# A two-layer graph attention kernel on one core: edge rows moved behind one-hots and merge on VectorE, and layer 1's gathered rows scaled chunk by chunk on ScalarE

## The chip, the core and the metric

One core of a Trainium2 chip. The metric is device time in microseconds of one execution; lower is better. The runs shown are whole executions, and the profile is one further execution of the same program.

## The reference

6250 nodes with 256 features, 200000 edges sorted by destination, 32 features an edge. A layer norm with relu, then two graph attention layers (4 heads of 64, then 1 head of 256) with self loops, and residual additions:

```python
def _gat(x, src, dst, ea, Wg, a_s, a_d, Wge, a_e, b, n, h, f):
    hx = (x @ Wg).reshape(n, h, f)
    he = (ea @ Wge).reshape(-1, h, f)
    al = leaky_relu(einsum('nhf,hf->nh', hx, a_s)[src] + einsum('nhf,hf->nh', hx, a_d)[dst]
                    + einsum('ehf,hf->eh', he, a_e), 0.2)
    m = segment_max(al, dst, num_segments=n)
    al = exp(al - m[dst])
    al = al / segment_sum(al, dst, num_segments=n)[dst]
    out = segment_sum(hx[src] * al[:, :, None], dst, num_segments=n)
    return out.reshape(n, h * f) + b

h = maximum(_layernorm(x), 0)
te = relu(edge_attr @ We0 + be0) * exp(h @ Wo0 + bo0)[src][:, None]
y = relu(_gat(h, *with_self_loops(src, dst, te), layer 0 weights) + h)
te = relu(edge_attr @ We1 + be1) * exp(y @ Wo1 + bo1)[src][:, None]
z = _gat(y, *with_self_loops(src, dst, te), layer 1 weights) + y
return x + (z + h)
```

## The kernel before

A prologue computes, per node, a table row for layer 0: the 256 projected features, the attention terms and the edge gate. Then the edges run in steps of 24 chunks of 128 edges, 66 steps a layer (the last two are shorter), first all of layer 0, then all of layer 1. Layer 0's node work writes the table that layer 1 gathers from.

All engines run lists written out by hand: each engine executes in the order in which `edges` issues, and waits only for what the data need. One pass of the loop in `edges` (line 668) handles step `st` and prepares the next one, `nx`:

- `gather(nx)`, line 871: 24 indirect DMAs issued by POOL, one a chunk, each bringing 128 table rows into `G`, a buffer of [128, 24, 270]. There are three of them, used in turn.
- `logits(st)`, lines 1071 to 1088 on VectorE: the first line that reads the gathered rows; it adds the edge terms from `rt` and `ade`, takes the leaky relu, and scans for the maximum of each segment. `ends` and `links` (lines 1099 to 1116) carry the maxima across rows.
- `spread`, `parts`, `blocks`, `rphase1`, `rphase2`, `adst` of `nx`: the edge network on TensorE and ScalarE (lines 968, 969, 977), and the destination's term (1029, 1043); the result stands in the PSUM tile `zad`.
- `maxima(st)`, lines 1126 to 1149: the softmax weights. ScalarE's Exp (line 1145) writes them to `k_w`, a part of the PSUM tile `kps`; VectorE copies them into `G` (line 1149).
- `scale(st)`, line 1180: VectorE multiplies all 24 gathered rows of `G`, 6144 elements a partition, by the weights in `k_w` (the 128 partitions hold 128 edges of each chunk).
- `carried(st)`, lines 1162 to 1170: VectorE adds, in row 0 of chunk 0, what a destination has from the step before (its tile `U`).
- `sums(st)`, line 1192: TensorE adds up the scaled rows by destination with one-hot matrices `S`, one fp32 multiplication a chunk, into the PSUM tile `u`. `evict(st)` (line 1197) copies it to `U` on ScalarE.
- `edge_rows(nx)`, lines 1057 and 1060: VectorE turns `zad` into `rt` by a transpose and reduces `ade` from it; the next step's `logits` read both.
- `onehots(nx)`, lines 1005 and 1008: VectorE compares, 3072 elements a partition, for the next `S`.
- `finish(pv)`: the merge of the step before with the self loop and the node's own values, on VectorE with one or two short ScalarE instructions: `nodes1` in layer 1 (lines 1213 to 1228 with the Exp in line 1222, then 1305 and 1307), `nodes0` in layer 0 (lines 1208 to 1242, then 1265 to 1279).
- `index_on`: in some passes, indices for later steps on VectorE (lines 602 to 633).

The order on VectorE around the change, in one pass:

```python
            drain(self.scale(st))
            self.carried(st)
            self.sums(st)
            if late:
                self.rows3(late)
                late = None
            self.edge_rows(nx)
            self.onehots(nx)
            if pv:
                drain(self.finish(pv))
            self.evict(st)
```

The last three steps of a layer are issued by `ending`, an order of its own; the pass before it (the one with `st["s"] + 4 == self.NS`) also finishes its own step.

Of the kernel before, what the change touches and what calls it, by code (L numbers as in the profile page):

```python
# [22 lines left out]
F32 = mybir.dt.float32  # L23
BF = mybir.dt.bfloat16
I32 = mybir.dt.int32
AF = mybir.ActivationFunctionType
# [5 lines left out]
P = 128  # L32
C = 24
SE = P * C
NX = 24
D = 256
# [43 lines left out]
class Kernel:  # L80
# [556 lines left out]
    def edges(self, ctx):  # L637
        nc = self.nc
        self.gp += [self.pool(f"gath{i}", 1, ctx) for i in range(1, 3)]
        self.sp = self.pool("onehot", 2, ctx)  # L640
        self.wp = self.pool("work", 2, ctx)
        self.np_ = self.pool("nodes", 2, ctx)
        self.xp = self.pool("index", 1, ctx)
        self.ps_y = self.pool("ps_y", 1, ctx, space=PSUM)
        self.ps_1 = self.pool("ps_1", 1, ctx, space=PSUM)
        self.ps_f = self.pool("ps_f", 1, ctx, space=PSUM)
        self.lf = self.ps_1.tile([P, 512], F32, name="lf")
        nc.vector.memset(self.lf[0:4, 0:1], -BIG)
        steps = self.steps
        self.state = {0: None, 1: None}  # L650
        self.nodes(steps[0])
        self.gather(steps[0])
        if self.NS % 2:
            self.load_lb(1)
        self.spread(steps[0])
        self.parts(steps[0])
        self.blocks(steps[0])
        drain(self.rphase1(steps[0]))
        self.load_ea(1)
        self.rphase2(steps[0])  # L660
        self.adst(steps[0])
        self.onehots(steps[0])
        drain(self.soon)
        self.edge_rows(steps[0])

        pv = late = None
        self.ahead, self.rest = 1, None
        for k, st in enumerate(steps):
            nx = steps[k + 1] if k + 1 < len(steps) else None
            if st["s"] + 2 >= self.NS:  # L670
                continue
            for q in steps[k + 1:k + 3]:
                if q["L"] is st["L"] and "tw" not in q:
                    self.nodes(q)
            self.load_lb(k + 2)
            left = 99
            if self.ahead < len(self.groups):
                left = self.groups[self.ahead][0] - 2 - (self.ahead + 2 >= len(self.groups)) - k
            if self.rest is None and left <= 2:
                gi = self.index_load(self.ahead, self.xp)  # L680
                self.rest = self.index_group(self.ahead, self.xp, gi)
            if st["s"] + 3 == self.NS:
                self.ending(st, *steps[k + 1:k + 3], pv, late, steps[k + 3] if k + 3 < len(steps) else None)
                pv = late = None
                continue
            self.gather(nx)
            drain(self.logits(st))
            self.ends(st)
            self.spread(nx)
            self.parts(nx)  # L690
            y = self.rphase1(nx)
            next(y)
            self.links(st)
            if late:
                self.rows2(late)
            self.load_fl(k + 1)
            self.blocks(nx)
            drain(self.maxima(st))
            drain(y)
            self.load_ea(k + 2)  # L700
            self.rphase2(nx)
            self.adst(nx)
            if "S" not in st:
                self.onehots(st)
            drain(self.scale(st))
            self.carried(st)
            self.sums(st)
            if late:
                self.rows3(late)
                late = None  # L710
            self.edge_rows(nx)
            self.onehots(nx)
            if pv:
                drain(self.finish(pv))
            self.evict(st)
            if pv:
                self.rows1(pv)
                late = pv
            self.index_on(left)
            if st["s"] + 4 == self.NS:  # L720
                drain(self.finish(st))
            if k >= 6:
                next(self.late, None)
                next(self.late, None)
            pv = st
        self.flag()

# [390 lines left out]
    def maxima(self, st):  # L1118
        nc, L, c, o, pc = self.nc, st["L"], st["C"], st["o"], st["pc"]
        H, G = L.H, st["G"]  # L1120
        V = nc.vector
        m = self.wp.tile([P, 4 * C], F32, name="m")
        t = self.mt
        n = H * c
        mh = m[:, :n].rearrange("p (h c) -> p h c", c=c)
        V.tensor_tensor(st["four"][:, :, n:2 * n].rearrange("p i (h c) -> p i h c", c=c),  # L1126
                        self.flpen[:, :, o:o + c].unsqueeze(2).to_broadcast([P, 2, H, c]),
                        self.lf[:, 160:224].rearrange("p (i h) -> p i h", i=2)[:, :, :H].unsqueeze(3)
                        .to_broadcast([P, 2, H, c]), op=OP.add)
        yield  # L1130
        V.tensor_reduce(m[:, :n], st["four"][:, :, :2 * n].rearrange("p i (j n) -> p n i j", j=2),  # L1131
                        axis=AX.XY, op=OP.max)
        yield
        V.tensor_sub(t[:, :n], st["al"][:, :n], m[:, :n])
        yield
        if st["prev"] is not None:
            pr = t[0:1, n:n + H]
            if H == 1:
                V.tensor_scalar(pr, pc[0:1, 0:H], mh[0:1, :, 0], -1e4, op0=OP.subtract, op1=OP.max)
            else:  # L1140
                V.tensor_sub(pr, pc[0:1, 0:H], mh[0:1, :, 0])
                yield
                V.tensor_scalar(pr, pr, -1e4, None, op0=OP.max)
            yield
        nc.scalar.activation(self.k_w[:, :n + H], t[:, :n + H], AF.Exp)
        V.tensor_tensor(G[:, :c, L.m:L.m + H].rearrange("p c h -> p h c"), mh,
                        self.isl[:, o:o + c].unsqueeze(1).to_broadcast([P, H, c]), op=OP.mult)
        yield
        V.tensor_copy(G[:, :c, L.p:L.p + H].rearrange("p c h -> p h c"),
                      self.k_w[:, :n].rearrange("p (h c) -> p h c", c=c))  # L1150
        yield
        st["pr"] = self.k_w[0:1, n:n + H]

    def carried(self, st):

# [17 lines left out]
    def scale(self, st, cuts=(0, C)):  # L1173
        nc, L, c = self.nc, st["L"], st["C"]
        H, G = L.H, st["G"]
        pw = self.k_w[:, :H * c].rearrange("p (h c) -> p c h", c=c)
        for c0, c1 in zip(cuts, cuts[1:]):
            c1 = min(c, c1)
            v = G[:, c0:c1, 0:D].rearrange("p c (h f) -> p c h f", h=H)
            nc.vector.tensor_tensor(v, v, pw[:, c0:c1, :].unsqueeze(3)  # L1180
                                    .to_broadcast([P, c1 - c0, H, L.F]), op=OP.mult)
            yield

    def sums(self, st, *parts):
        nc, L, c = self.nc, st["L"], st["C"]
        G, S = st["G"], st["S"]
        for a, b in parts or ((0, c),):
            for i in range(a, b):
                j = st["n"] = st.get("n", -1) + 1
                if j == 0:  # L1190
                    st["u"] = self.ps_1.tile([P, 512], F32, name="u")
                nc.tensor.matmul(st["u"][:, :L.W], S[:, i, :], G[:, i, 0:L.W], start=(j == 0), stop=(j == c - 1))  # L1192
# [263 lines left out]
def drain(g):  # L1456
    for _ in g:
        pass
# [93 lines left out]
```

## Time and profile before

| | us |
|---|---|
| median of 3 runs | 4064.29 |
| lowest and highest | 4062.84, 4064.88 |
| the profiled execution, its own time | 4068.59 |
| its span, first to last instruction | 4066.2 |

How to read the lines: a group of instructions is given by line of the kernel, engine, operation and tiles (out<-in), shapes, count; then busy time in us and the mean of one in ns; then the engine's idle time just before these instructions and what ended it. A line of the timeline gives start, duration (us), then the same names, and in brackets the idle time before it with what released it. Two rows on one engine may overlap, since instructions are pipelined. A line of a query by source line gives the least, median and largest duration in ns. A line of the stages gives the stretch, its length, POOL's busy time and count, then the granted TensorE clock, the DMA share and GB/s. PE is TensorE, PEld its weight load, DVE VectorE, ACT ScalarE, POOL GpSimd, SP SyncE.

### The profile page before, as it was taken

To read this page: it belongs to the slowest core of one execution; us is meant where nothing else is said; L and a number is where in the kernel's file an instruction comes from. 1 tells how busy PE (TensorE), PEld (TensorE's weight loads), DVE (VectorE), ACT (ScalarE), POOL (GpSimd) and SP (SyncE) were. 2 spreads that over 40 slices of the span, in tenths; PEclk is the share of its full clock that TensorE was granted. 3 is DMA by queue.
4 is the path that set the end of the run, shared out by engine and by line. 5 is a ranking of instruction groups with operands and counts; after the bars stand their busy time and mean duration, and the time that the engine had idled before them with its cause. 6 is when DMAs were issued, how large, how long until landed. Compare 5 with 4: busy or idle time off the path is not lost.

```text
span 4066.2 us, 34155 instructions
## 1 busy us (share of the span) xinstructions
PE 2696.3 (66%) x9878; PEld 1737.4 (43%) x9878; DVE 2855.0 (70%) x6188; ACT 519.9 (13%) x1158; POOL 3012.7 (74%) x3255
## 2 busy tenths in 40 slices
PE   8776666666666766766646656666657666666665
PEld 6454444444444444444433433433434334334334
DVE  7887877877877877777856656656566566565666
ACT  5211111111111111111110000000000000000000
POOL 5777777777777777777747777777777777777775
PEclk9888888887887788888777787777777777777777
DMA  7455555555555555555434455455455445445443
GB/s 251 137 152 140 146 149 140 145 149 144 142 150 147 140 148 147 141 147 148 134 103 133 136 142 141 130 141 140 132 140 140 134 137 143 132 137 142 132 137 96
DMA packets 231085, 576.17 MB, mean 142 GB/s; under 512 B 63097, under 2 KB 87871, under 8 KB 230825
## 3 DMA queue, kind: packets, MB, share of 16 engines
q0 software_dynamic: 150144, 422.75, 39.6%
q1 hardware_dynamic: 80331, 150.52, 11.4%
q8 instruction: 79, 1.29, 0.1%
q14 instruction: 115, 0.94, 0.1%
q10 hardware_dynamic: 416, 0.67, 0.1%
HBM read 542.72 MB, written 31.09 MB: 141 GB/s over the span
## 4 chain that ended last, share of the span: by engine, by line
POOL 53%; issue 19%; DVE 19%; DMA 4%; PE 4%; ACT 1%; SPq 0%; DVEq 0%; ACTq 0%; POOLq 0%
POOL G L871 53%; DVE G L1180 6%; DMA G<-T,src 4%; DVE S L1008 3%; DVE lb L992 1%; PE ps L444 1%; PE y L968 1%; PE u L1192 1%; DVE rt L1057 1%; DVE m L1131 1%; DVE ade L1060 0%; DVE G L1169 0%; DVE fb L1126 0%; DVE al L1075 0%; DVE al L1073 0%
## 5 line engine op out<-in xcount | busy, mean ns | idle before, releaser
L871 POOL DMA_INDIRECT G<-T,src x3102 | 2959.9, 954 | 1001.1 <-issue 929.7
L1192 PE MATMUL u<-G,S 128*128 128x270 f32 (+1 forms) x6252 | 1617.9, 423 | 250.8 <-DVE G L1170 247.2
L1192 PEld LDWEIGHTS u<-G,S 128*128 128x128 f32 x6252 | 1295.4, 209 | 585.6 <-DVE G L1170 314.7
L1180 DVE TENSOR_TENSOR G<-G,kps 128x6144 f32<-128x6144 f32 (+2 forms) x140 | 853.3, 6099 | 0.0
L1071 DVE TENSOR_TENSOR G<-rt,G 128x96 f32<-128x96 f32 (+1 forms) x132 | 30.3, 229 | 910.3 <-DMA G<-T,src 910.0
L1099 PE MATMUL lf<-ident,fb 128*36 128x128 f32 (+1 forms) x132 | 49.5, 375 | 710.8 <-DVE fb L1088 684.3
L1008 DVE TENSOR_TENSOR S<-kps,loc 128x3072 f32<-128x3072 f32 x132 | 437.5, 3315 | 4.6
L968 PE MATMUL y<-ea,webd 64*128 64x256 f32 (+1 forms) x1056 | 396.7, 846 | 51.4 <-ACT R L969 51.4
L977 PE MATMUL zad<-R,wea 128*64 128x384 f32 (+1 forms) x1056 | 301.2, 711 | 158.4 <-ACT R L969 158.1
L969 ACT ACTIVATE R<-y,webd 128x1024 f32<-128x1024 f32 (+2 forms) x264 | 235.6, 892 | 1226.0 <-PE y L968 741.5
L1099 PEld LDWEIGHTS lf<-ident,fb 128*36 128x36 f32 (+1 forms) x132 | 15.6, 118 | 752.5 <-DVE fb L1088 725.2
L977 PEld LDWEIGHTS zad<-R,wea 128*64 128x64 f32 x1056 | 86.7, 185 | 426.0 <-ACT R L969 340.6
L968 PEld LDWEIGHTS y<-ea,webd 64*128 64x128 f32 x1056 | 125.6, 291 | 125.5 <-ACT R L969 70.4
L1197 ACT ACTIVATE U<-u 128x270 f32<-128x270 f32 (+1 forms) x132 | 51.9, 394 | 645.9 <-PE u L1192 645.9
L1029 PE MATMUL zad<-a,Q 128*128 128x12 bf16 (+1 forms) x132 | 26.1, 198 | 160.1 <-DVE a L1024 160.1
L444 PE MATMUL fin<-wg,h1T 128*128 128x260 f32 x264 | 128.7, 638 | 3.7 <-ACT h1T L1287 3.7
L1057 DVE STREAM_TRANSPOSE rt<-zad 128x768 f32<-128x768 f32 (+1 forms) x130 | 124.5, 957 | 5.1 <-PE zad L1043 5.1
L992 DVE TENSOR_TENSOR lb<-lb,kps 128x1536 bf16<-128x1536 bf16 (+1 forms) x68 | 113.5, 1670 | 0.0
L1222 ACT ACTIVATE mw<-mw,mg 128x2 f32<-128x2 f32 x66 | 19.7, 298 | 623.9 <-DVE mg L1221 623.9
L1029 PEld LDWEIGHTS <-Q 128*128 128x128 bf16 x132 | 16.0, 121 | 172.7 <-DVE a L1024 165.8
L1043 PE MATMUL zad<-lb,aq 128*128 128x384 bf16 (+1 forms) x264 | 86.5, 421 | 0.0
L444 PE MATMUL ps<-wg,hT 128*128 128x266 f32 x292 | 83.2, 410 | 1.7 <-ACT hT L326 1.6
(190 smaller groups left out, 2109.8 us busy)
## 6 DMA issues: line engine op xcount, KB each, us to landing
G<-T,src POOLq DMA_INDIRECT x3102, 2.8
ea<-in_ea_dram SPq DMA_DIRECT2D x64, 768.0 KB
lb<-locrow SPq DMA_DIRECT2D x64, 384.0 KB
T<-t1row SPq DMA_DIRECT2D x66, 227.5 KB
tw<-T SPq DMA_DIRECT2D x66, 225.8 KB
tw<-T SPq DMA_DIRECT2D x66, 117.2 KB
tw<-in_x_dram SPq DMA_DIRECT2D x66, 112.0 KB
out_dram<-fb SPq DMA_DIRECT2D x64, 112.0 KB
```

Source lines behind the costliest of these rows:

```text
L444: self.nc.tensor.matmul(ps[:, :L.MW], hT[:, k, :], self.wg[L.l][:, k, :], start=(k == 0), stop=(k == 1))
L871: nc.gpsimd.indirect_dma_start(out=G[:, c, 0:L.TW], out_offset=None, in_=self.rows[L.l][0:n * (1 + L.l), :], in_offset=bass.IndirectOffset ...
L968: nc.tensor.matmul(y[:, i, :n], self.webd[l][r, :], ea[r, w], start=True, stop=True)
L969: nc.scalar.activation(R[:, :, w], y[:, :, :n], AF.Relu, bias=self.be[l])
L977: nc.tensor.matmul(st["zad"][i * PH:(i + 1) * PH, o], self.wea[l][0], R[:, i, w], start=True, stop=False)
L992: V.tensor_tensor(lb[:, :, :n], lb[:, :, :n], self.k_part.unsqueeze(2).to_broadcast([P, i, n]), op=OP.is_equal)
L1008: nc.vector.tensor_tensor(st["S"][:, c0:c1, :], self.k_iota.unsqueeze(1).to_broadcast(w), self.loc[:, o + c0:o + c1].unsqueeze(2).to_broad ...
L1043: self.nc.tensor.matmul(st["zad"][:, o], st["aq"].rearrange("p k j -> p (k j)"), st["lb"][:, w], start=False, stop=True)
L1057: V.transpose(rv[:, :32 * c].rearrange("p (b n) -> p b n", b=2), z.rearrange("p (b n) -> p b n", b=2)[:, :, :16 * c])
L1099: self.nc.tensor.transpose(self.lf[0:e.shape[1], 1:P + 1], e, self.ident)
L1180: nc.vector.tensor_tensor(v, v, pw[:, c0:c1, :].unsqueeze(3) .to_broadcast([P, c1 - c0, H, L.F]), op=OP.mult)
L1192: nc.tensor.matmul(st["u"][:, :L.W], S[:, i, :], G[:, i, 0:L.W], start=(j == 0), stop=(j == c - 1))
```

## The change

Two things. In layer 1, in all steps but those of `ending`, the weights go to a tile `kw` in SBUF instead of `k_w` in PSUM, and ScalarE multiplies the gathered rows, one instruction of 128x256 a chunk with the chunk's column of `kw` as its scale, in place of VectorE's one instruction. And in both layers `edge_rows(nx)` is issued behind the one-hots, the merge of `pv`, the eviction and the index work; in the pass ahead of `ending` that step's own merge follows it.

```diff
             self.gather(nx)
+            st["rows"] = st["L"].l
             drain(self.logits(st))
...
-            drain(self.scale(st))
+            if st["rows"]:
+                self.scale_rows(st)
+            else:
+                drain(self.scale(st))
             self.carried(st)
             self.sums(st)
             if late:
                 self.rows3(late)
                 late = None
-            self.edge_rows(nx)
             self.onehots(nx)
             if pv:
                 drain(self.finish(pv))
...
             self.index_on(left)
-            if st["s"] + 4 == self.NS:
-                drain(self.finish(st))
             if k >= 6:
                 next(self.late, None)
                 next(self.late, None)
+            self.edge_rows(nx)
+            if st["s"] + 4 == self.NS:
+                drain(self.finish(st))
             pv = st
...
-        nc.scalar.activation(self.k_w[:, :n + H], t[:, :n + H], AF.Exp)
+        k_w = self.k_w
+        if st.get("rows"):
+            st["w"] = k_w = self.wp.tile([P, C + 1], F32, name="kw")
+        nc.scalar.activation(k_w[:, :n + H], t[:, :n + H], AF.Exp)
...
         V.tensor_copy(G[:, :c, L.p:L.p + H].rearrange("p c h -> p h c"),
-                      self.k_w[:, :n].rearrange("p (h c) -> p h c", c=c))
-        yield
-        st["pr"] = self.k_w[0:1, n:n + H]
+                      k_w[:, :n].rearrange("p (h c) -> p h c", c=c))
+        yield
+        st["pr"] = k_w[0:1, n:n + H]
...
+    def scale_rows(self, st):
+
+        G = st["G"]
+        for c in range(st["C"]):
+            v = G[:, c, 0:D]
+            self.nc.scalar.activation(v, v, AF.Copy, scale=st["w"][:, c:c + 1])
```

## The prediction

> **What bounds the kernel now.** I read the page's busy shares first, then the groups of instructions by line with what ended the idle time before them, then the stages, and then the timeline of one step of each layer.
>
> ```profile
> PE 2696.3 (66%) x9878; PEld 1737.4 (43%) x9878; DVE 2855.0 (70%) x6188; ACT 519.9 (13%) x1158; POOL 3012.7 (74%) x3255
> ```
> ```profile
> POOL G L871 53%; DVE G L1180 6%; DMA G<-T,src 4%; DVE S L1008 3%; DVE lb L992 1%; PE ps L444 1%; PE y L968 1%; PE u L1192 1%; DVE rt L1057 1%; DVE m L1131 1%; DVE ade L1060 0%; DVE G L1169 0%; DVE fb L1126 0%; DVE al L1075 0%; DVE al L1073 0%
> ```
> ```profile
> L871 POOL DMA_INDIRECT G<-T,src x3102 | 2959.9, 954 | 1001.1 <-issue 929.7 <-DMA T<-t1row 40.5 <-DMA T<-trow 12.5
> L1180 DVE TENSOR_TENSOR G<-G,kps 128x6144 f32<-128x6144 f32 (+2 forms) x140 | 853.3, 6099 | 0.0
> L1071 DVE TENSOR_TENSOR G<-rt,G 128x96 f32<-128x96 f32 (+1 forms) x132 | 30.3, 229 | 910.3 <-DMA G<-T,src 910.0
> ```
> ```profile
> L871 POOL DMA_INDIRECT G<-T,src x3102: 942/947/1197, 88.8 to 4036.3; - x194
> ```
>
> By busy share three engines look alike. The groups part them. Nearly all of POOL's idle time before a gather, 929.7 of 1001.1 us, is "issue": 0.30 us each, POOL's own way from one gather to the next. The rest is mainly the two waits for tables (40.5 between the layers, 12.5 at the start). VectorE on the other hand stands 910 us at L1071, the first line that reads gathered rows, until a gather lands. The account closes: 88.8 us before the first gather, 2959.9 + 1001.1 - 12.5 for the gathers (the 12.5 lies in the 88.8), 29 from the last one (4036.3) to 4066.2, together 4066. So the time is 3102 gathers at 954 + 300 ns, a head, a wait between the layers and a tail. DVE, ACT and PE decide only in the last three, or where they reach POOL.
>
> **The change, part by part.** Here is a step of layer 1.
>
> ```profile
> 3012.05 0.20 DVE L1071 TENSOR_TENSOR G<-rt,G 128x24 f32<-128x24 f32 x1 [10.01 <-DMA G<-T,src]
> ...
> 3016.05 0.20 ACT L1145 ACTIVATE kps<-mt 128x25 f32<-128x25 f32 x1 [0.30 <-DVE mt L1139]
> ...
> 3016.38 6.55 DVE L1180 TENSOR_TENSOR G<-G,kps 128x6144 f32<-128x6144 f32 x1
> ...
> 3017.93 1.11 ACT L969 ACTIVATE R<-y,webd 128x1024 f32<-128x1024 f32 x1 [1.68 <-PE y L968]
> ...
> 3021.85 0.82 PE L1043 MATMUL zad<-lb,aq 128*128 128x384 bf16 x2
> ...
> 3022.96 0.48 DVE L1162 SCALAR_TENSOR_TENSOR G<-U,kps,G 1x257 f32<-1x257 f32 x1
> ...
> 3023.49 0.96 DVE L1057 STREAM_TRANSPOSE rt<-zad 128x768 f32<-128x768 f32 x1
> ...
> 3023.62 12.58 PE L1192 MATMUL u<-G,S 128*128 128x261 f32 x48 [0.95 <-DVE G L1170]
> 3024.49 0.23 DVE L1060 TENSOR_REDUCE ade<-rt 128x24 f32<-128x72 f32 x1
> 3024.64 0.15 DVE L1005 COPY kps<-lastloc 128x1 f32<-128x1 f32 x1
> ...
> 3024.82 3.36 DVE L1008 TENSOR_TENSOR S<-kps,loc 128x3072 f32<-128x3072 f32 x1
> ...
> 3029.05 0.30 ACT L1222 ACTIVATE mw<-mw,mg 128x2 f32<-128x2 f32 x1 [10.01 <-DVE mg L1221]
> ...
> 3029.38 0.22 DVE L1224 SCALAR_TENSOR_TENSOR mg<-U,mw 128x1 f32<-128x1 f32 x1 [0.37 <-ACT mw L1222]
> ...
> 3030.61 0.48 DVE L1307 SCALAR_TENSOR_TENSOR fb<-tw,mw,fb 128x256 f32<-128x256 f32 x1
> ...
> 3036.24 0.39 ACT L1197 ACTIVATE U<-u 128x261 f32<-128x261 f32 x1 [6.90 <-PE u L1192]
> ...
> 3040.30 0.20 DVE L1071 TENSOR_TENSOR G<-rt,G 128x24 f32<-128x24 f32 x1 [9.20 <-DMA G<-T,src]
> ...
> 3048.56 1.11 ACT L969 ACTIVATE R<-y,webd 128x1024 f32<-128x1024 f32 x1 [1.77 <-PE y L968]
> ```
>
> *Removed:* one L1180 of 6.55 us in each of layer 1's 63 ordinary steps (66 less the three that the end handles by itself), 412 us of VectorE. None of it is worth anything directly: behind it VectorE waits for a gather all the same, 10.01 us in the row above, 9.20 in the next. That wait becomes longer.
>
> *Added:* 63 x 24 = 1512 scalings of 128x256 on ScalarE, which reads one per-row factor. The trace has no such instruction. Its neighbours, the first without and the second with two per-row operands:
>
> ```profile
> L1271 ACT ACTIVATE fb<-fb 128x256 f32<-128x256 f32 x66 | 27.5, 417 | 129.2 <-DVE fb L1269 129.2
> L1253 ACT ACTIVATE hw<-tw 128x256 f32<-128x256 f32 x66 | 38.6, 585 | 0.2 <-issue 0.2
> ```
> ```profile
> 1001.59 0.40 ACT L1197 ACTIVATE U<-u 128x270 f32<-128x270 f32 x1 [4.14 <-PE u L1192]
> 1001.88 0.38 ACT L1287 ACTIVATE h1T<-fin 128x256 f32<-128x256 f32 x1
> ```
>
> One operand stands half way, 0.50 us. Two that follow each other overlap by 0.11 us (1001.59 + 0.40 against 1001.88), so I take a row each 0.39 to 0.40 us and 0.585 as the upper bound: 9.6 us a step, at most 14.0. The Trainium skill (ScalarE: Activation LUTs, "What ACT_TABLE_LOAD costs") gives 186 ns plus 0.833 ns an element, 93 ns more for each pointer operand and 93 ns of overlap; as an estimate from that page a row would be 0.49 us and a step 9.6, which the trace's neighbours bear out.
>
> The rows queue behind ScalarE's L969, which ends at 3019.04, so they end at 3028.6 (bound: 3033.1). The first is done near 3019.5 and lets L1162 go 3.4 us earlier than now. PE gains less: its L1043 runs until 3022.67 in front of the sums, so they start 0.9 us earlier; PE needs 12.58 us for them, more than ScalarE needs for the rows, and ends about 3035.3 (by the bound no later than 3034 + the last chunk). U is then copied a little earlier than at 3036.24, and G comes free no later.
>
> *The new wait:* L1222 stands behind the 24 rows on ScalarE, and VectorE waits for it at L1224. Queued there are the rest of the merge and, now, the edge rows. The merge ends 1.7 us after L1224 starts (L1307 ends 3031.09) and the edge rows take 1.15 us (3023.49 to 3024.64). VectorE is then through at 3028.6 + 0.3 + 2.9, about 3032, at most 3036.4. The next gather lands for 3040.3: a margin of 8 us, at worst 4. It costs nothing.
>
> *Moved:* edge rows, in both layers. L1057 and L1060 issue no DMA and pass nothing on SP or POOL; they pass one-hots, merge and the index work on VectorE, and in the last ordinary step they go ahead of that step's own merge, which waits for U anyway. In layer 0 the same work is done later in the same step, in front of an idle stretch:
>
> ```profile
> 1018.93 0.96 DVE L1057 STREAM_TRANSPOSE rt<-zad 128x768 f32<-128x768 f32 x1
> ...
> 1020.29 0.15 DVE L1005 COPY kps<-lastloc 128x1 f32<-128x1 f32 x1
> ...
> 1032.37 0.26 DVE L1071 TENSOR_TENSOR G<-rt,G 128x96 f32<-128x96 f32 x1 [3.63 <-DMA G<-T,src]
> ```
>
> Cost nothing, cover 3.63 us; without that cover 1.36 us a step. The merge comes 1.36 us earlier.
>
> **What can reach POOL** is then the length of a gather, median 947 and mean 954 ns. The stages show more in layer 0 (1400.87 / 1464 = 957) than in layer 1 (951), and the timeline shows where it comes from.
>
> ```profile
> 120.00:1970.00 1850.00, 1400.87 (x1464) 0.83 0.53 145
> 2100.00:3990.00 1890.00, 1431.53 (x1505) 0.74 0.50 137
> ```
> ```profile
> 2902.83 0.48 DVE L1162 SCALAR_TENSOR_TENSOR G<-U,kps,G 1x257 f32<-1x257 f32 x1
> 2902.96 1.17 POOL L871 DMA_INDIRECT G<-T,src  x1 [0.30 <-issue]
> ```
> ```profile
> 1026.62 0.42 DVE L1265 TENSOR_TENSOR fb<-U,mw 128x256 f32<-128x256 f32 x1
> 1026.69 1.16 POOL L871 DMA_INDIRECT G<-T,src  x1 [0.30 <-issue]
> ```
>
> A VectorE instruction with two SBUF inputs that runs across a gather's start holds it: L1162 ends 0.35 us after that start, and the gather is 0.22 us longer than 947; L1265 likewise 0.35 and 0.21. So about the first 0.13 us are free and the rest is paid. L1180, with kps in PSUM as its second input, runs from 3016.38 to 3022.93 across the starts of five gathers, these two and three between them, and leaves them as they are.
>
> ```profile
> 3017.30 0.95 POOL L871 DMA_INDIRECT G<-T,src  x1 [0.30 <-issue]
> ...
> 3022.32 0.94 POOL L871 DMA_INDIRECT G<-T,src  x1 [0.30 <-issue]
> ```
>
>  The Trainium skill (SBUF - State Buffer, "Who interferes with whom") has it so: a VectorE instruction with two SBUF inputs contends with a GpSimd instruction that reads SBUF, and one with a single SBUF input does not. By that rule, and the trace agrees, taking L1180 away frees no POOL time.
>
> The excess is 10 ns x 1538 = 15 us in layer 0 and 4 ns x 1542 = 6 us in layer 1. The change moves these instructions against the gathers' beat of 1.25 us. Layer 0: 1.36 us earlier is one beat and 0.11 us, so in the step above L1265 would end 0.24 after the start and cost 0.11 instead of 0.21. If each of the 63 steps won that 0.10, 6 us; I take half, -3. Layer 1: L1162 now starts by ScalarE's first row, L1305 and L1307 by its last. A 0.48 us instruction hits when it starts 0.11 to 0.36 us ahead of a gather, 0.25 in 1.25 of the cases, and costs 0.12 on average: three of them, 63 steps, 5 us in place of 6, so -1.
>
> The weights move from PSUM into an SBUF tile, so the copy L1149 becomes SBUF to SBUF. Nearest row, a one-input SBUF instruction with 24 elements:
>
> ```profile
> L1096 DVE TENSOR_SCALAR src<-src x66: 146/151/356, 129.4 to 2043.6; 128x24 int32<-128x24 int32 x64, 128x14 int32<-128x14 int32 x1, 128x13 int32<-128x13 int32 x1
> ```
>
> It is sometimes stretched to 0.36 us, so VectorE is the one that waits: nothing for POOL; if POOL paid the whole 0.15 us in each step, +9. The same section of the Trainium skill (SBUF - State Buffer) says that copies in a two-port mode and GpSimd block each other fully, whoever starts first; by that rule the +9 is the end to fear.
>
> Sum: -3 - 1 = -4 us on the profiled execution's 4068.59 (span 4066.2 and 2.4 around it), 4064.6. That execution lies 4.3 above the median of the runs, 4064.29; on the median it is 4060.
>
> **Rivals.** *The chain as a bill.* It gives L1180 6%, 244 us, and VectorE's share is 70%: if VectorE were the bound, layer 1 would lose up to 412 us and end near 3652. Against it: the 910 us at L1071 and POOL's 0.30 us. 1%.
>
> *Hits vanish.* If the moved instructions miss the gathers, up to 15 + 6 = 21 us go: 4043. It decides how many of 126 steps hit; over 8 us need that 40% of the excess goes. 14%.
>
> *Hits multiply* (slower). L1162 and the pair L1305 and L1307 each land 0.11 us ahead of a gather in every layer 1 step: 63 x 2 x 0.25 = 31 in place of 6, with the copy's 9 at most +34, 4098. The point: a start 0.11 to 0.36 us ahead of a gather. All phases are locked to the landing of gathered rows, so a bad one repeats. Over 8 us: 6%.
>
> *ScalarE overruns* (slower). From L1071 to the end of L969 are 7.0 us, in steps that load locations 9.4 (3040.30 to 3049.67); with 24 r + 3.5 behind it a step exceeds 30.1 us when r passes 0.77 us on average. At r = 1.0 a step takes 35.7 us: 63 x 5.6 = 353, 4417. The bound 0.585 speaks against it. 2%.
>
> **How the numbers follow.** About 0.2%, 8 us, is what a measurement of this kernel can tell from no change. Forecast (within 8 us) 77%, faster 15% (1 + 14), slower 8% (6 + 2). Range: from the median of 4064, down 11 to 4053 with half of the excess gone, up 9 to 4073 with the copy paid and no gain in the beat.
>
> **What would show it.** Right: gathers still 0.30 us apart from "issue", mean 947 to 958 ns; the wait at L1071 over 1100 us; L1180 x77; 1512 new ACT rows of 0.50 us; L1222 behind them. Wrong: POOL waiting for anything of PE or ACT, L1071 without a wait in layer 1, rows over 0.77 us, or gathers in layer 1 over 970 ns.

## The result, and the profile after

Over 12 runs of each, the changed kernel takes 4053.3 us at the median (4048.77 to 4055.68), the kernel before 4064.14 (4059.49 to 4066.95). The ratio is 0.9974, with a 95% interval from 0.9966 to 0.9982: 0.26% faster, 10.8 us. The prediction was 4060 with a range from 4053 to 4073: the time lies 0.3 us inside the lower edge. The likeliest case, "within 8 us" (77%), did not come; what came is the case "faster" (15%), by the rival "hits vanish", of which about half came true.

The page of the changed kernel: busy shares, and the chain by line. `gather` is now line 875, VectorE's scale 1187, the new scale on ScalarE 1196, `logits` start at 1075.

```profile
PE 2638.1 (65%) x9878; PEld 1725.2 (43%) x9878; DVE 2442.3 (60%) x6125; ACT 1117.5 (28%) x2670; POOL 2996.7 (74%) x3255
```
```profile
POOL G L875 30%; DVE G L1187 9%; ACT G L1196 8%; DMA G<-T,src 8%; PE y L972 4%; DVE S L1012 4%; PE u L1206 2%; DVE lb L996 2%; PE ps L444 1%; DVE m L1135 1%; DVE rt L1061 1%; ACT R L973 1%; DVE al L1079 1%; DVE al L1077 1%; DVE fb L1092 1%
```

VectorE lost 413 us of work (2855.0 to 2442.3), ScalarE took on 598, and the span moved by 15 (4066.2 to 4051.4). The chain looks quite different, POOL's gathers 53% before and 30% now, and yet the time is made in the same way. Several engines wait for one another here, and the chain is followed through whichever came last; its shares were no bill for the parts before and are none now. The groups by line say it better:

```profile
L875 POOL DMA_INDIRECT G<-T,src x3102 | 2944.0, 949 | 1003.3 <-issue 914.8 <-DMA T<-t1row 40.0 <-DMA T<-trow 14.4
L1196 ACT ACTIVATE G<-G,kw 128x256 f32<-128x256 f32 x1512 | 608.9, 497 | 0.0
L1187 DVE TENSOR_TENSOR G<-G,kps 128x6144 f32<-128x6144 f32 (+3 forms) x77 | 441.0, 5736 | 0.0
```

The 3102 gathers were busy for 2959.9 us, now 2944.0: 15.9 less. The idle time between them is the same to 2.2 us, and so are the head and the tail (first gather 89.3, last 4021.1, end 4051.4). The whole change of the profiled span, 14.8, is in the length of the gathers, 954 ns before and 949 now. In the traces, gathers longer than 975 ns had 14.4 us over 947 in layer 0 (144 of them) and 6.7 in layer 1 (64); now 7.3 (77) and 3.2 (28). I call this sum the excess of a layer below. It accounts for 10.6 of the 15.9 us. The other 5.3 lie in the gathers up to 975 ns, whose mean fell from 947.4 to 945.6 ns, and they are not shown to come from the change: the same changed kernel, profiled once more (below), has 946.9. The medians, over 12 runs each, differ by 10.8.

Where VectorE's 413 us went is a question for the waits of VectorE: who waited for whom, in us, how often, and the longest in us:

```profile
DVE G L1075 <- DMA G<-T,src: 859.9, 121, 20.3
DVE mg L1238 <- ACT mw L1236: 281.2, 65, 4.5
DVE G L1169 <- ACT G L1196: 186.3, 62, 3.3
```

They became waits for ScalarE, 281 us in the merge behind the 24 rows (23.8 before) and 186 for the first row (none before), while the wait for gathers fell by 50. Here is a step of layer 1 in the timeline:

```profile
3000.41 0.20 DVE L1075 TENSOR_TENSOR G<-rt,G 128x24 f32<-128x24 f32 x1 [9.31 <-DMA G<-T,src]
...
3006.25 1.11 ACT L973 ACTIVATE R<-y,webd 128x1024 f32<-128x1024 f32 x1 [1.64 <-PE y L972]
3007.26 9.67 ACT L1196 ACTIVATE G<-G,kw 128x256 f32<-128x256 f32 x24
...
3007.79 0.48 DVE L1169 SCALAR_TENSOR_TENSOR G<-U,kw,G 1x257 f32<-1x257 f32 x1 [2.96 <-ACT G L1196]
...
3010.79 11.20 PE L1206 MATMUL u<-G,S 128*128 128x261 f32 x48
...
3017.15 0.22 DVE L1238 SCALAR_TENSOR_TENSOR mg<-U,mw 128x1 f32<-128x1 f32 x1 [4.53 <-ACT mw L1236]
...
3018.79 0.98 DVE L1061 STREAM_TRANSPOSE rt<-zad 128x768 f32<-128x768 f32 x1
...
3019.80 0.23 DVE L1064 TENSOR_REDUCE ade<-rt 128x24 f32<-128x72 f32 x1
3022.03 0.39 ACT L1211 ACTIVATE U<-u 128x261 f32<-128x261 f32 x1 [4.91 <-PE u L1206]
3028.69 0.20 DVE L1075 TENSOR_TENSOR G<-rt,G 128x24 f32<-128x24 f32 x1 [8.65 <-DMA G<-T,src]
```

The step runs as it was laid out, and ends 8.65 us before its gather, as it used to end 9 or 10 before it.

### The profile page after: what moved, and what is told of

Its sections match the earlier page's. It is cut to its first block, busy times and chain, and to the rows that moved or that the text cites. A ratio compares the mean times of both kernels' runs of the same rounds, so it can differ in the third digit from the quotient of the medians.

```text
span 4051.4 us, 37118 instructions
## 1 busy us (share of the span) xinstructions
PE 2638.1 (65%) x9878; PEld 1725.2 (43%) x9878; DVE 2442.3 (60%) x6125; ACT 1117.5 (28%) x2670; POOL 2996.7 (74%) x3255
## 4 chain that ended last, share of the span: by engine, by line
POOL 30%; DVE 29%; issue 13%; ACT 9%; PE 9%; DMA 8%; DVEq 0%; SPq 0%; ACTq 0%; POOLq 0%
POOL G L875 30%; DVE G L1187 9%; ACT G L1196 8%; DMA G<-T,src 8%; PE y L972 4%; DVE S L1012 4%; PE u L1206 2%; DVE lb L996 2%; PE ps L444 1%; DVE m L1135 1%; DVE rt L1061 1%; ACT R L973 1%; DVE al L1079 1%; DVE al L1077 1%; DVE fb L1092 1%
## 5 line engine op out<-in xcount | busy, mean ns | idle before, releaser
L875 POOL DMA_INDIRECT G<-T,src x3102 | 2944.0, 949 | 1003.3 <-issue 914.8
L1206 PE MATMUL u<-G,S 128*128 128x270 f32 (+1 forms) x6252 | 1577.8, 415 | 197.3 <-DVE G L1177 194.0
L1196 ACT ACTIVATE G<-G,kw 128x256 f32<-128x256 f32 x1512 | 608.9, 497 | 0.0
L1187 DVE TENSOR_TENSOR G<-G,kps 128x6144 f32<-128x6144 f32 (+3 forms) x77 | 441.0, 5736 | 0.0
L1238 DVE SCALAR_TENSOR_TENSOR mg<-U,mw 128x1 f32<-128x1 f32 x66 | 14.6, 222 | 281.2 <-ACT mw L1236 281.2
L1169 DVE SCALAR_TENSOR_TENSOR G<-U,kw,G 1x257 f32<-1x257 f32 x62 | 29.4, 475 | 186.3 <-ACT G L1196 186.3
L1311 ACT ACTIVATE t1row<-t1row 128x1 f32<-128x1 f32 x66 | 13.4, 203 | 351.8 <-DVE t1row L448 351.8
```

What stands on the lines that cost most here:

```text
L875: nc.gpsimd.indirect_dma_start(out=G[:, c, 0:L.TW], out_offset=None, in_=self.rows[L.l][0:n * (1 + L.l), :], in_offset=bass.IndirectOffset ...
L1187: nc.vector.tensor_tensor(v, v, pw[:, c0:c1, :].unsqueeze(3) .to_broadcast([P, c1 - c0, H, L.F]), op=OP.mult)
L1196: self.nc.scalar.activation(v, v, AF.Copy, scale=st["w"][:, c:c + 1])
```

## The experiments

The theory: POOL's gathers, back to back, are the time, and the change acts only by how often a VectorE instruction with two SBUF inputs lies across the start of a gather. Rival A: less work on VectorE is what speeds up the gathers. Rival B: the step's chain became shorter. Differences in us are of medians, against the kernel before as it was measured beside each, unless something else is named.

**The two parts alone.** Only the edge rows moved:

```diff
-            st["rows"] = st["L"].l
+            st["rows"] = 0
```

> The changed kernel with layer 1's rows scaled by VectorE again: only the edge rows are moved. Theory (gathers are the whole time, and what changes is how often VectorE's two-SBUF-input instructions lie across a gather's start): layer 0 as in the changed kernel, its gathers' mean down from 957 to 952 ns, -7 us; in layer 1 the merge moves 1.36 us against a beat of 1.25, its share of the excess falls from 4.5 to about 2, -3; together -10 us. Rival A (less VectorE work in layer 1 gives the gain): layer 0 and 1 unchanged, 0. Rival B (the step's chain is shorter): 0, nothing on the chain is shorter.

Measured: ratio 0.9986 (0.9977 to 0.9995), 5.1 us faster. In the profiled execution layer 0's excess is 9.7 us (14.4 before), layer 1's 6.7 as before. Layer 0 did what was expected in two thirds of the size. Layer 1 gained nothing, and I see the reason in my number: I moved its merge by 1.36 us, layer 0's time for the edge rows, but in layer 1 they take 1.15 (3023.49 to 3024.64 in the prediction's timeline). That is 0.10 short of the beat of 1.25 instead of 0.11 beyond it. The reckoning moves the merge through the steps of a trace and adds up what its instructions would then lengthen; for the kernel before, moved by 1.2 to 1.1 us, it gives 7 to 11 us, not 2. This was worked out afterwards, and no run of its own tests it.

Only the scaling on ScalarE, with the edge rows in their old place:

```diff
+            self.edge_rows(nx)
             self.onehots(nx)
...
-            self.edge_rows(nx)
             if st["s"] + 4 == self.NS:
```

> The changed kernel with the edge rows back ahead of the one-hots: only the scaling goes to ScalarE. Theory: layer 0 as before, 957 ns, 0 us; in layer 1 L1162 starts by the first scaled row and the merge by the last, as in the changed kernel, so its gathers fall from 952.5 to about 949 ns, -6 us; together -6. The two parts add up to the whole within 5 us. Rival A: the whole gain, -11 us, and all of it in layer 1.

Measured: 0.9996 (0.9987 to 1.0005), 1.6 us faster, not clear of nothing. Excess 14.3 us in layer 0, as before, and 3.4 in layer 1, near the changed kernel's 3.2: the place was right, the total smaller than the 6 expected. Rival A wanted the whole gain here and does not get it, although this kernel has all of VectorE's relief. The parts sum to 6.7 us against 10.8 for the whole, which the intervals of 3 to 4 us to each side allow.

**The suspected cost taken away, in both kernels.** The order of the groups on VectorE stays; one input of each wide instruction of the merge (128x256) moves from SBUF to PSUM. In layer 0 the four additions are also put in another order, the last weights go to PSUM, and ScalarE writes the relu a second time. The core of the edit, cut:

```diff
+            wq, hw = self.kps[:, i:i + 8].rearrange("p (i h) -> p i h", i=2), self.lf[:, D:2 * D]
...
+            V.tensor_add(nrow, xw, hw)
+            yield
+            V.tensor_add(hw, a, hw)
+            yield
+            V.tensor_add(b, b, hw)
...
+            V.tensor_add(nrow, nrow, hw)
...
+            q = self.lf[:, D:2 * D]
+            self.nc.scalar.activation(q, xw, AF.Copy)
...
-        V.scalar_tensor_tensor(o, U[:, 0:D], w[:, 0, 0:1], xw, op0=OP.mult, op1=OP.add)
-        yield
-        V.scalar_tensor_tensor(o, tw[:, 0:D], w[:, 1, 0:1], o, op0=OP.mult, op1=OP.add)
+        t = q if "k" in st else o
+        V.scalar_tensor_tensor(t, U[:, 0:D], w[:, 0, 0:1], q, op0=OP.mult, op1=OP.add)
+        yield
+        V.scalar_tensor_tensor(o, tw[:, 0:D], w[:, 1, 0:1], t, op0=OP.mult, op1=OP.add)
```

> The kernel before, with one input of each wide merge instruction put in PSUM (layer 0: the weights, hw and the sums go through PSUM, ScalarE writes the relu twice; layer 1: ScalarE copies xw to PSUM, the first sum stays there); order and VectorE's work as before. Theory: the hits of the merge vanish (9.4 us in layer 0, 4.4 in layer 1 in the trace of before), those of the carried rows stay: -13 us, gathers' mean 949 to 950 ns in layer 0. Rival A and B: no change, VectorE does the same work and ScalarE a little more.

Measured: 0.9971 (0.9959 to 0.9982), 12.6 us faster, where 13 were expected. Excess 4.4 and 3.3 us. Two of the merge's groups in this kernel, with nearly the same VectorE time (424 and 484 ns in the kernel before):

```profile
L1271 DVE TENSOR_TENSOR fa<-tw,kps 128x256 f32<-128x256 f32 x66 | 27.7, 420 | 2.2
L1328 DVE SCALAR_TENSOR_TENSOR lf<-U,mw,lf 128x256 f32<-128x256 f32 x66 | 32.3, 489 | 2.6 <-PE lf L1116 0.3
```

> The changed kernel with the same inputs in PSUM. Theory: of its excess of 10.5 us (7.3 and 3.2 in the two layers) the merge's part goes, 4.8 and 2.9: 8 us below the changed kernel, near 4046, 19 below the kernel before. Rival A and B: as the changed kernel.

Measured on the changed kernel: 0.9956 (0.9943 to 0.997) of the kernel before, 4044.78 us, 18.4 faster than before and 8.5 faster than the changed kernel; 8 were expected. Excess 3.9 and 0.6. This is the fastest version of the study. The gathers of both kernels, first before's, then the changed one's:

```profile
L871 POOL DMA_INDIRECT G<-T,src x3102 | 2948.7, 951 | 1003.9 <-issue 930.1 <-DMA T<-t1row 42.0 <-DMA T<-trow 14.3
```
```profile
L875 POOL DMA_INDIRECT G<-T,src x3102 | 2937.1, 947 | 1002.8 <-issue 921.1 <-DMA T<-t1row 41.9 <-DMA T<-trow 14.1
```

Neither rival has a reason for these two: VectorE's work is the same and ScalarE's a little more. Gather by gather it is plainer still. I counted the gathers that start at least 0.05 us into a wide instruction of the merge which then runs on for more than 0.15 us. In the kernel before these are 129, and 128 of them took over 975 ns; in the changed kernel 70, and 69 did. With one operand in PSUM they are 85 and 63, and not one took more than 960 ns.

**VectorE work added, to shift the phase.** In the changed kernel, ahead of layer 0's merge, copies with one input, in PSUM. The first of three such kernels has one copy of 208 elements:

```diff
             self.onehots(nx)
+            for _ in range(1 * (st["L"].l == 0)):
+                nc.vector.tensor_copy(self.padt[:, 0:2, :], self.kps[:, 0:104].unsqueeze(1).to_broadcast([P, 2, 104]))
             if pv:
```

The other two have three copies each, of 324 and of 258 elements.

> The changed kernel with one VectorE copy of 208 elements from PSUM (one input, none in SBUF) ahead of layer 0's merge, about 0.30 us a step, 19 us of VectorE work in all. Theory: it moves the merge to where it lies worst against the beat of the gathers; carrying the shift through the steps of the changed kernel's trace, layer 0's excess after the one-hots goes from 5 to 17 us: +13 us against the changed kernel, layer 0's gathers at 961 ns. Rivals A and B: VectorE has 3.6 us of slack a step, 0.

Measured: 0.9995 (0.9986 to 1.0004) of the kernel before, 9.4 us above the changed kernel's median, where 13 were expected. Layer 0's excess is 16.9 us; 14.0 of it lie behind the one-hots, the part for which 17 was worked out. A shift of 0.28 us a step (the copy takes 0.36 and overlaps its neighbours), with over 3 us of slack, takes back nearly the whole gain.

> The same with three such copies of 324 elements, about 1.25 us a step, one beat of the gathers, 79 us of VectorE work in all. Theory: the merge lies as in the changed kernel: 0 us against the changed kernel (within 4, because the beat need not be met exactly), so four times the added work costs less than in the run with 0.30 us. Rival B (the chain counts): slower than the 0.30 run.

Measured: 0.9993 (0.9984 to 1.0002), 6.9 us above the changed kernel, where 0 was expected. The timeline shows why:

```profile
1026.42 1.54 DVE L718 COPY padt<-kps 128x324 f32<-128x324 f32 x3
...
1027.88 0.14 DVE L1225 TENSOR_SCALAR cnt<-U 128x1 f32<-128x1 f32 x1
```

The copies moved the merge by 1.46 us, not 1.25. That is 0.21 us beyond the beat, and there the reckoning gives 16 us; layer 0's excess was 18.4, 14.1 of it behind the one-hots. So I had built another bad phase, not the good one, and made the copies smaller:

> The three copies ahead of layer 0's merge again, but of 258 elements each: the trace of the run with 324 shows that they moved the merge by 1.46 us, not 1.25, 0.21 us past the beat, where the carried-over steps of the changed kernel's trace give 16 us of excess (18 were measured). With 66 elements less each the shift is 1.46 - 3 x 0.069 = 1.25 us. Theory: layer 0's excess falls back to 5 to 9 us and the time to the changed kernel's, within 4 us, with 79 us more VectorE work. Rivals A and B (added VectorE work or a longer chain costs): as the run with 324, 7 us or more above the changed kernel.

> The changed kernel once more, as the measure for the run with the copies of 258 on the same chip: 4053 us, layer 0's excess 7, layer 1's 3.

Measured together: 0.9976 (0.9966 to 0.9986) with the copies, 0.9973 (0.9962 to 0.9984) for the changed kernel without them, medians 4058.49 and 4056.8. The copies now shift the merge by 1.26 us, and with three and a half times the added work of the first of these kernels (81 us of copies against 23) nearly the whole gain is back. Layer 0's excess fell from 18.4 to 11.7 us (8.8 in the changed kernel beside it), where 5 to 9 were expected; but 5.1 of the 11.7 lie ahead of the one-hots, which the copies do not move, and behind them are 6.6 (5.3). (The profiled executions of the 208 and the 324 run lie 10 and 13 us above their medians, and their gathers up to 975 ns take 948.3 ns on the mean; so their excess is compared among profiles only.)

**Layer 1 without any scaling.** In the kernel before, gathered rows unscaled in layer 1's ordinary steps:

```diff
-            drain(self.scale(st))
+            if st["L"].l == 0:
+                drain(self.scale(st))
             self.carried(st)
```

> The kernel before without L1180 in layer 1's ordinary steps: the gathered rows there stay unscaled, nothing takes the work over, 412 us of VectorE go. Theory: nothing directly; only the phases in layer 1 change (L1162 6.5 us earlier, the merge by the edge rows, which wait for TensorE): -4 to +4 us against the kernel before, layer 0 at 957 ns as before. Rival A (VectorE's work weighs on the gathers): at least the changed kernel's gain in layer 1, -7 or more. If VectorE were the bound of layer 1: -400.

Measured: 1.0003 (0.9993 to 1.0012), 1.0 us slower. That is no change clear of noise: 409 us of VectorE work gone are worth nothing. Its waits:

```profile
DVE G L1072 <- DMA G<-T,src: 968.2, 123, 20.3
DVE rt L1058 <- PE zad L1044: 356.7, 65, 6.4
```

The time went into the wait of the edge rows for TensorE (357 us, before 5.1) and the wait for gathers (58 more). Layer 1's excess is 9.0 us where A needed a fall of 7 or more from 6.7, so rival A falls. That it rose is little beyond scatter: layer 0, which this edit does not touch, has 16.3 for 14.4. The first of the two waits also shows what the new place of the edge rows avoids, 173 us in the kernel with only the scaling moved and 8.5 in the changed one; it is idle time, and by itself worth nothing.

**One gather of 24 replaced**, in each layer 1 step, by a plain load on SP's queue (chunk 11 then holds other rows; the lines that leave out its gather are cut):

```diff
+        if L.l:
+            nc.sync.dma_start(G[:, 11, 0:L.TW], self.T[1][0:P, 0:L.TW])
```

> The changed kernel with one of 24 gathers of each layer 1 step replaced by a plain load of 128 table rows on SP's queue, so that chunk 11 holds other rows. Theory: 66 gathers less on POOL, 1.25 us each: -82 us against the changed kernel, the rest as it is. Rival B (the chain of a step bounds layer 1 as well): clearly less than 82.

Measured: 0.9791 (0.9776 to 0.9806) of before; 75 us below the changed kernel by the medians of two separate series, 79 by the spans of the profiles (4051.4 and 3972.3). Expected were 82. Layer 1's stretch of gathers is 80 us shorter, with 2 us more of excess in it: together the 82. Layer 0 has another 2 us more of excess; the rest of what is missing in the medians is not explained, with four runs of this kernel. A step with 1.25 us less on POOL became about that much shorter altogether, which leaves B no ground.

**Side by side,** all but the kernel with a gather less. Excess by the traces in us, layer 0's in two parts, ahead of and behind the one-hots of a step:

| kernel | time against before | layer 0 ahead | layer 0 behind | layer 1 |
|---|---|---|---|---|
| before | | 3.9 | 10.5 | 6.7 |
| changed | -10.8 | 2.2 | 5.1 | 3.2 |
| changed, once more | -10.8 | 3.5 | 5.3 | 3.1 |
| only edge rows moved | -5.1 | 2.8 | 6.9 | 6.7 |
| only the scaling | -1.6 | 3.1 | 11.2 | 3.4 |
| before, operand in PSUM | -12.6 | 4.1 | 0.3 | 3.3 |
| changed, operand in PSUM | -18.4 | 3.5 | 0.4 | 0.6 |
| copies, shift 0.28 | -0.6 | 2.8 | 14.0 | 2.7 |
| copies, shift 1.46 | -3.1 | 4.3 | 14.1 | 3.1 |
| copies, shift 1.26 | -9.1 | 5.1 | 6.6 | 2.6 |
| layer 1 unscaled | +1.0 | 5.7 | 10.6 | 9.0 |

The change of the summed excess, one profile each, agrees with the change of the medians within 3.5 us in every row. Layer 0's part ahead of the one-hots has the same order in all of them; its 2.2 to 5.7 us show how far the excess scatters by itself.

## Why the prediction was right, point by point

*The number.* It held by 0.3 us. The lower bound was worked out as half of the excess gone, and that is what came: 21.1 us to 10.5. The forecast itself, 4 us, was less than half of the gain.

*POOL bounds, VectorE's 412 us are free.* Right: the change, the run without scaling (1.0003) and the run with a gather less say the same from three sides. 

*ScalarE's rows.* Right: 497 ns (0.50), 9.67 us a step (9.6).

*The step's layout.* Right: L1169 3.5 us earlier against the start of `logits` (3.4), TensorE only about 1 (10.4 us after `logits` start, before 11.6), and a margin of 8.65 (8). The sums also became shorter, 11.2 us for 12.6.

*Edge rows cost nothing.* Right as a cost. The prediction had their time right in both layers, 1.36 and 1.15 us; the expectation of the first experiment then took 1.36 for layer 1 too. In the whole change that shift does not count, since layer 1's merge hangs on ScalarE's last row.

*What reaches POOL: -3 and -1.* The mechanism was right and the terms too small. Layer 0 was worked out as 6 us "if each step won that" and then halved without a reason: the excess fell by 7.1, 5.4 of it behind the one-hots, where the change acts, and the rest within the scatter. It was also not L1265, the row shown, that won most, but the merge's last addition (L1279 before, L1293 now): 43 gathers lengthened by 4.3 us in all, now 14 by 1.0. Layer 1 (it has 1563 gathers, not 1542) was taken by chance hits, 5 in place of 6; but its phases are locked to the landing of the gathers, and repeat. They fell well, by 3.5: the carried row went from 2.4 to 0.3 us, the pair's first instruction from 2.9 to 1.0, and its second rose from 1.4 to 1.9. The prediction gave this 1 us, by averages; that the phases fell so well is luck. Both layers together are 10.6 us, beside 10.8 by the medians.

*The copy from the SBUF tile.* The value taken was right, 0 of at most 9. 58 of the 63 copies overlap a gather, and none of these gathers is longer than 962 ns. That does not show such a copy to be harmless: only 9 of them lay across a gather's start, and none ran on for more than 0.12 us, less than the 0.13 us that the instructions with two SBUF inputs have free as well. The copy by its source line, least, median and largest duration:

```profile
L1156 DVE COPY G<-kw x63: 187/190/332, 2101.1 to 3964.5; 128x24 f32<-128x24 f32 x63
```

In a few steps it is itself stretched to 0.33 us. By the Trainium skill (SBUF — State Buffer, "Who interferes with whom") copies in a two-port mode and GpSimd block each other. For this copy only VectorE was seen to wait.

*The markers.* One was wrong: the wait at the first line of `logits` was to pass 1100 us and fell to 860. The slack did not stay there; it went to the places where VectorE now waits for ScalarE.

## What to carry to other kernels

Before a busy engine is relieved, look at what it waits for in the stage concerned: 412 us of VectorE work stood in front of a wait for gathers, and removing 409 of them with nothing in their place moved nothing. When one engine issues back to back all the time, look at the spread of its own instructions: the difference between the mean of 954 ns and the median of 947 was all that could be won here without touching the gathers. And where two engines run in a locked rhythm, a small shift repeats in every step (0.28 us a step cost 9 us here); instead of hunting for the good phase, take away what collides, here by one operand in PSUM.

## What the runs showed of the hardware

A gather is lengthened by a VectorE instruction with two SBUF inputs that is under way when the gather starts, from 0.13 us after the start to the end of that instruction, up to 0.25 us. The instruction must have begun early enough: in the kernel before, 28 times the carried row (L1162) started less than 0.106 us ahead of a gather; then the gather kept its length and L1162 took up to 0.56 us instead of 0.48. The 15 that started 0.108 us or more ahead and lengthened their gather took 0.48. In the changed kernel, layer 0, an instruction of the merge that starts 0.21 us ahead of a gather and ends 0.21 after its start makes it 0.07 longer than 947 ns:

```profile
1022.48 0.42 DVE L1279 TENSOR_TENSOR fb<-U,mw 128x256 f32<-128x256 f32 x1
1022.69 1.02 POOL L875 DMA_INDIRECT G<-T,src  x1 [0.30 <-issue]
```

I had not expected that the same instructions with one operand in PSUM would be free of it to this extent (layer 1's excess of 3.2 us to 0.6), at the same time on VectorE. But one input in SBUF is not always free. In the changed kernel with operands in PSUM, three casts from SBUF to SBUF that started 0.05 to 0.08 us ahead of a gather lengthened it, to 0.99, 1.02 and 1.03 us:

```profile
1201.31 0.25 DVE L602 CAST gf<-gi 128x192 f32<-128x192 int32 x1
1201.36 1.03 POOL L875 DMA_INDIRECT G<-T,src  x1 [0.30 <-issue]
```

And ScalarE scales gathered chunks at 0.40 us each in sequence beside running gathers. All 1512 of these instructions overlap a gather, and none took more than 0.51 us. The 515 gathers of layer 1 beside them have a median of 946 ns, as have the 1048 others.
